# Another order of one period's operations in a convolution and Fourier-mixing kernel on one core

## The chip, the cores and the metric

The kernel runs on one core of one Trainium2 chip. A core has five engines that follow their own instruction streams: TensorE (PE in the profile; its weight loads appear as PEld), VectorE (DVE), ScalarE (ACT), GpSimd (POOL) and SyncE (SP). They meet at semaphores. The metric is the device time of one execution in microseconds (us); lower is better.

## The reference

Two layers on x, 4 x 256 x 256 x 64, all in float32. The change touches layer 0 alone:

```python
h = _pw(_ln(x, g1, b1), w_te, b_te)
F = jnp.fft.fft2(h.astype(jnp.complex64), axes=(1, 2))
fr = jnp.concatenate([jnp.real(F), jnp.imag(F)], axis=-1)
fc = jax.nn.gelu(_pw(fr, w_fc, b_fc), approximate=False)
re, im = (fc[..., :HID], fc[..., HID:])
sp = jnp.real(jnp.fft.ifft2(re + 1j * im, axes=(1, 2)))
x1 = x + _pw(sp, w_tp, b_tp)
h2 = _pw(_ln(x1, g2, b2), w_fe, b_fe)
d = lax.conv_general_dilated(h2, w_dw, window_strides=(1, 1), padding='SAME', dimension_numbers=('NHWC', 'HWIO', 'NHWC'), feature_group_count=HID) + b_dw
d = jax.nn.gelu(d, approximate=False)
return x1 + _pw(d, w_fp, b_fp)
```

`_ln` is a layer normalisation over the 64 channels and `_pw` a matrix product over channels. Layer 1 adds a moving average along time and a truncated Fourier mixing of it; the kernel does that with one 256 x 256 matrix per channel, after layer 0 has ended.

## The kernel before

**Three streams.** Layer 0 is cut into three streams of small operations, each with a short name in the code. A *stream index* says to which piece of the data an instance belongs.

- Forward transform (names in f, and y0, y1, yt0, yt1): loads x, normalises it, folds it by symmetry, and multiplies it on PE with Fourier tables along the first image axis. fx is the scaling by the reciprocal deviation (xt, POOL, line 410), fh0 and fh1 the POOL half sums (xb, line 609, after DVE's lines 582 and 602), y0 and y1 the PE products (line 615), yt0 and yt1 their evictions by ACT (line 633).
- Spectral pairs (x, xs, m, gc, b, g, p, z, zs, w, zt, and u, us, uc, uf for the way back): the second axis of the transform (x, line 725), the mixing of spectra with its GELU (m and p on PE, line 750; b on DVE, line 770; gc on ACT, line 764; g on ACT, line 775), the folding of its result (p0 and p1, POOL, line 781), the products with w_tp (z, PE, line 805), transposes (zt, PE, line 823, with an ACT copy at line 833), and the inverse transform (u, PE, line 856; evictions us, uc and uf at lines 873, 887, 888 and 907).
- Convolution chunks, 128 in number, 32 for an image: load x and u, add the inverse transform (s, PE, line 1041; r0 and r1, DVE, lines 1054 and 1062), normalise (cx: xn, POOL, line 410), transpose (t0 and t1, PE, line 1088; tt0 and tt1, ACT, lines 1098 to 1100), form sums of neighbouring rows (T0: POOL, lines 1124, 1125, 1128; T1: POOL, lines 1131 and 1132; written to td), multiply by the convolution's weights, combine, apply GELU (a0, a1: ACT, line 1276), multiply by w_fp (o0, o1: PE, line 1283), transpose back (ft, line 1308), add and store (st, DVE, line 1322).

**The products of a chunk.** The 3x3 convolution and the product before it are merged into six sums of products. `products` (line 1166) does the 128-row part and `products_beside` (line 1180) the 64-row part. The six are split in two: FIRST (k 1, 2, 3, 4; operations gm and gh) and REST (k 0, 5; operations em and eh). In FIRST, k 1 and 2 go to two single PSUM banks ("FIRST singles", tiles ps_h_c with a 1 in the name) and k 3 and 4 to one double tile, the *pair* (ps_hh_c), of which there is a single buffer. REST goes to two single banks (tiles ps_h_c with a 0). The sums leave PSUM as follows: evict_rest (ec, ACT, line 1200), evict_first (gc_, ACT, lines 1209 and 1212), combine_first (cf0: DVE, lines 1233 and 1234; cf1: DVE, lines 1239 to 1245), add_sums (sp, POOL, lines 1218 and 1223). Line 1245 is the last to read the pair.

**Normalisation.** Forward groups and chunks share one computation of the reciprocal deviation: a seed by integer arithmetic (DVE, line 315), and Newton steps in which ACT squares (lines 354, 364, 375, 395, 396) and POOL multiplies (lines 355, 365, 376, 397). Its result scales xt and xn at line 410.

**What sets the order.** All compute engines run in the order in which the program emits their instructions (a manual schedule, kept in order); DMAs are issued from SP's queue and, for the final output, from ACT's. The program emits in *periods*. `period(n)` goes through a list of names with offsets and calls `do(op, n + offset)`, so that em:-4 in period n is the REST product of chunk n-4 and is the same instance as em:-3 one period before. `do` emits every instance up to the index that hasn't been emitted, and first those that it depends on by two tables, FOLLOWS and EARLY. Before an operation that needs PSUM banks, `make_room` emits what frees one. The place of a name in the list is therefore a wish; what lands on an engine also depends on these tables.

There are four lists. SPECTRUM runs without chunks; FULL (line 1585) runs while all three streams are active, in 60 periods from n = 72 to 131, which emit chunks 0 to 58 (one period, at the border between the first image and the second, has none); MIXED takes over when the forward stream is done, and CONV when only chunks are left. In the trace FULL covers about 824 to 2370 us. `period` selects so:

```python
names = FULL if n < B * FWD + 4 else MIXED if n < CONV_FROM else CONV
```

In FULL the three streams' statistics are done jointly, and some names of the list (fC, fp, fA and others of the forward statistics) emit nothing, as the chunk's operation does their part.

Of the kernel before, what the change touches and what calls it, by code (L numbers as in the profile page):

```python
# [136 lines left out]
def conv_seq_kernel(ctx: ExitStack, tc: tile.TileContext, a: dict, tables: bass.AP, out: bass.AP):  # L137
    nc = tc.nc
    x = a["x"]
# [11 lines left out]
        x="xs", m0="b0", m1="b1", z="zs", w="zt", u="uc", s="r1", t0="tt0", t1="tt1", gm="cf0",  # L151
        em="ec1", o0="fs0", o1="fs1", ft0="st0", ft1="st1", y0="yt0", y1="yt1",
# [1421 lines left out]
    def numbered(text):  # L1574

        return [(w.split(":")[0], int(w.split(":")[1]) if ":" in w else 0) for w in text.split()]

    follows = {}
    for line in FOLLOWS.replace("\n", "|").split("|"):
# [3 lines left out]


    FULL = numbered("""
        g1:-3 em:-4 b0:-2 ec1:-4 cm:-1 gh:-4 m0:-1 ec0:-4 fh1:-3 gc_0:-4 cf0:-4 a0:-5 g0:-2 m1:-1
        p0:-3 fq:-1 p1:-3 z:-3 gc1:-1 fr:-1 gc0:-1 fs0:-5 o0:-5 o1:-5 b1:-1 fa:-3 fs1:-5 fh0:-3
        b0:-1 y0:-3 ft0:-5 g1:-2 fR:-1 sp0:-4 cx:-2 w:-4 ft1:-5 st0:-5 zs:-3 p0:-2 fC:-3 yt0:-3
        cc:-1 xl fm:-1 p1:-2 t1:-2 ul tt1:-2 sp1:-4 fp:-2 fM:-1 s cl fl t0:-2 w:-3 fA:-2 st1:-5
        gc_1:-4 fx:-2 r0 XL tt0:-2 r1 cM:-1 uf:-3 zs:-2 gc1 T0:-2 T1:-2 m1 UL:1 fB:-2 y1:-3 cA:-1 cr  # L1590
        g0:-1 yt1:-3 u:-2 x:2 b1 zt:-4 us:-2 zt:-3 m0 xs:2 cf1:-4 z:-2 x:1 xs:1 gc0 a1:-4 Ta:-2
        cB:-1 fb:-2 cq gm:-3 cC:-1 uc:-2 cR cp:-1 eh:-3
    """)

    MIXED = numbered("""
# [204 lines left out]
```

## Time and profile before

| | us |
|---|---|
| median of 3 runs | 4286.83 |
| lowest and highest | 4285.57, 4288.68 |
| the profiled execution's own time | 4282.18 |
| its span | 4280.0 |
| stage of list FULL, in the trace | about 824 to 2370 |
| one period in its steady part (spacing of DVE's line 1054) | 26.50 |
| one period of MIXED, steady | 23.57 |

The profile is of one execution. Its page gives the busy time of each engine, the chain of work that ended last, and the costliest groups of instructions; the trace can be asked for waits (which instruction of which engine waited for which other, and for how long), for a timeline of one engine and for tables by window. In a timeline the columns are start, duration, engine, line, operation, output and inputs, shapes, the number of merged instructions, and in brackets the idle time ahead with what ended it. The granted TensorE clock of the run was 0.987 of full speed. The costliest groups of the page show how the work is spread:

```profile
L770 DVE TENSOR_TENSOR g<-ps_p,g 128x512 f32<-128x512 f32 x1040 | 703.0, 683 | 127.7 <-ACT g L764 109.4
L781 POOL TENSOR_TENSOR g<-g 128x512 f32<-128x512 f32 (+1 forms) x520 | 674.1, 1312 | 92.8 <-ACT g L775 84.9
L775 ACT ACTIVATE g<-g,b_fc 128x1024 f32<-128x1024 f32 (+1 forms) x520 | 595.2, 1145 | 1.7 <-DVE g L770 1.6
L750 PE MATMUL ps_p<-xs,wp 64*128 64x512 f32 (+1 forms) x2080 | 562.2, 615 | 7.0 <-DVE g L770 3.8
L1166 PE MATMUL ps_h_c<-td,wc_main 128*128 128x256 f32 x2048 | 500.5, 387 | 3.7 <-DVE g L770 1.4
```

After the count come the busy time and the mean duration in ns, and then the idle time of the engine ahead of these instructions with its main releaser.

### The profile page before, as it was taken

To read this page: it belongs to the slowest core of one execution; us is meant where nothing else is said; L and a number is where in the kernel's file an instruction comes from. 1 tells how busy PE (TensorE), PEld (TensorE's weight loads), DVE (VectorE), ACT (ScalarE), POOL (GpSimd) and SP (SyncE) were. 2 spreads that over 40 slices of the span, in tenths; PEclk is the share of its full clock that TensorE was granted. 3 is DMA by queue.
4 is the path that set the end of the run, shared out by engine and by line. 5 is a ranking of instruction groups with operands and counts; after the bars stand their busy time and mean duration, and the time that the engine had idled before them with its cause. 6 is when DMAs were issued, how large, how long until landed. Compare 5 with 4: busy or idle time off the path is not lost.

```text
span 4280.0 us, 67389 instructions
## 1 busy us (share of the span) xinstructions
PE 4123.3 (96%) x22443; PEld 2329.5 (54%) x22443; DVE 3453.5 (81%) x5234; ACT 2962.3 (69%) x5409; POOL 3174.2 (74%) x3156
## 2 busy tenths in 40 slices
PE   8999999889999999899999999999998899999999
PEld 4544444345555555455555556666665566654444
DVE  6968999889999999899999878888886799962222
ACT  3438988778888887788888777888885466641221
POOL 6869999789999988899988877888886688840000
PEclk9999999999999999999999999999999999999999
DMA  6664555535555545445554333444433544439895
GB/s 192 213 192 132 158 159 165 170 99 138 139 138 138 138 138 141 125 132 140 141 141 133 100 106 101 110 108 123 109 99 101 165 114 114 118 109 368 344 342 226
DMA packets 763904, 655.26 MB, mean 153 GB/s; under 512 B 46413, under 2 KB 657695, under 8 KB 755240
## 3 DMA queue, kind: packets, MB, share of 16 engines
q1 hardware_dynamic: 726696, 583.84, 47.0%
q10 hardware_dynamic: 36864, 67.13, 4.1%
q8 instruction: 180, 2.95, 0.3%
q14 instruction: 164, 1.34, 0.1%
HBM read 364.81 MB, written 286.00 MB: 152 GB/s over the span
## 4 chain that ended last, share of the span: by engine, by line
PE 47%; DVE 8%; DMA 2%; POOL 2%; ACT 1%; issue 1%; SPq 0%; DVEq 0%; POOLq 0%; ACTq 0%
PE ps_o L1504 9%; PE ps_h_c L1166 5%; PE ps_p L750 4%; PE ps_h_c L1180 4%; PE ps_f_c L1283 4%; PE ps_s_c L1041 3%; PE ps_hh_c L1166 3%; PE ps_z L805 3%; PE ps_u L856 2%; PE ps_x L725 2%; PE ps_t_c L1088 2%; PE ps_ft_c L1308 2%; PE ps_hh_c L1180 2%; PE ps_zt L823 1%; PE ps_y L615 1%
## 5 line engine op out<-in xcount | busy, mean ns | idle before, releaser
L770 DVE TENSOR_TENSOR g<-ps_p,g 128x512 f32<-128x512 f32 x1040 | 703.0, 683 | 127.7 <-ACT g L764 109.4
L781 POOL TENSOR_TENSOR g<-g 128x512 f32<-128x512 f32 (+1 forms) x520 | 674.1, 1312 | 92.8 <-ACT g L775 84.9
L775 ACT ACTIVATE g<-g,b_fc 128x1024 f32<-128x1024 f32 (+1 forms) x520 | 595.2, 1145 | 1.7 <-DVE g L770 1.6
L750 PE MATMUL ps_p<-xs,wp 64*128 64x512 f32 (+1 forms) x2080 | 562.2, 615 | 7.0 <-DVE g L770 3.8
L1166 PE MATMUL ps_h_c<-td,wc_main 128*128 128x256 f32 x2048 | 500.5, 387 | 3.7 <-DVE g L770 1.4
L1504 PE MATMUL ps_o<-xc,mt 128*128 128x512 f32 x1024 | 441.2, 594 | 2.6 <-DVE oc L1518 2.6
L1166 PEld LDWEIGHTS ps_h_c<-td,wc_main 128*128 128x128 f32 x2048 | 372.6, 192 | 99.3 <-issue 32.1
L764 ACT COPY g<-ps_p 128x512 f32<-128x512 f32 (+1 forms) x520 | 298.5, 589 | 163.3 <-PE ps_p L750 80.7
L1276 ACT ACTIVATE h_c<-h_c,b_conv 128x1024 f32<-128x1024 f32 x256 | 296.5, 1160 | 158.1 <-DVE h_c L1245 53.8
L1518 DVE TENSOR_SCALAR oc<-ps_o,b_fp 128x512 f32<-128x512 f32 x128 | 93.6, 749 | 348.0 <-DMA out_dram<-oc 177.4
L1516 ACT ACTIVATE oc<-ps_o,b_fp 128x512 f32<-128x512 f32 x128 | 86.4, 686 | 359.4 <-PE ps_o L1504 202.8
L1128 POOL TENSOR_TENSOR td<-tt 128x512 f32<-128x512 f32 x256 | 326.9, 1298 | 10.0
L1504 PEld LDWEIGHTS ps_o<-xc,mt 128*128 128x128 f32 x1024 | 194.9, 191 | 248.3 <-issue 236.2
L609 POOL TENSOR_TENSOR xb<-xt 128x512 f32<-128x512 f32 x224 | 284.9, 1279 | 54.9 <-DVE xt L602 36.6
L750 PEld LDWEIGHTS ps_p<-xs,wp 64*128 64x128 f32 x2080 | 191.7, 186 | 235.7 <-issue 84.2
L805 PE MATMUL ps_z<-g,w_tp 128*64 128x512 f32 x1024 | 284.7, 616 | 25.8 <-POOL g L781 13.9
L1322 DVE TENSOR_TENSOR st<-x_c,ps_ft_c 128x256 f32<-128x256 f32 x512 | 260.5, 599 | 36.9 <-PE ps_ft_c L1308 36.8
L725 PEld LDWEIGHTS ps_x<-tab,yb 128*64 128x64 f32 x4064 | 232.7, 137 | 95.7 <-issue 38.3
L1180 PE MATMUL ps_h_c<-td,wc_half 64*128 64x256 f32 (+1 forms) x2048 | 278.9, 396 | 2.3 <-POOL td L1132 1.0
L615 PE MATMUL ps_y<-xb,tab 128*64 128x512 f32 x1024 | 270.6, 614 | 10.8 <-POOL xb L609 9.2
L1283 PE MATMUL ps_f_c<-h_c,w_fp 128*64 128x512 f32 x1024 | 266.1, 614 | 15.2 <-ACT h_c L1276 15.2
L1041 PE MATMUL ps_s_c<-uc_c,tab 64*128 64x512 f32 x1024 | 260.4, 612 | 16.6 <-DVE uc_c L990 11.2
(201 smaller groups left out, 9588.2 us busy)
## 6 DMA issues: line engine op xcount, KB each, us to landing
y_d<-yt SPq DMA_DIRECT2D x256, 256.0 KB, 3.6
yb<-y_d SPq DMA_DIRECT2D x256, 256.0 KB, 4.2
u_d<-ut SPq DMA_DIRECT2D x256, 256.0 KB, 3.6
x_c<-in_x_dram SPq DMA_DIRECT2D x512, 128.0 KB, 3.6
x_d<-st SPq DMA_DIRECT2D x128, 512.0 KB, 5.1
xc<-x_d SPq DMA_DIRECT2D x64, 1024.0 KB, 8.3
out_dram<-oc ACTq DMA_DIRECT2D x256, 256.0 KB, 5.7
xt<-in_x_dram SPq DMA_DIRECT2D x504, 128.0 KB, 2.5
```

What stands on the lines that cost most here:

```text
L725: nc.tensor.matmul(ps[r * C : (r + 1) * C, j * N + t * P : j * N + (t + 1) * P], blk[:, t, k, r * C : (r + 1) * C], tb[:, t, :], start=Tru ...
L750: nc.tensor.matmul(ps[:, :nf], wp[rows, cols], rhs[rows], start=True, stop=r == 1 or not pr["special"],)
L770: nc.vector.tensor_tensor(gt[:, i], re, gt[:, 1], op)
L775: nc.scalar.activation(g, g, AF.Gelu, bias=b_fc[:, half : half + 1])
L781: nc.gpsimd.tensor_tensor(g[:, 0], g[:, 0], g[:, 1], op)
L805: nc.tensor.matmul(ps[r * C : (r + 1) * C, :nf], w_tp, d[:, :nf], start=True, stop=True)
L1041: nc.tensor.matmul(pss[i], tb[i * C : (i + 1) * C], uc[i * C : (i + 1) * C, ::-1, 1 - r, :] if down else uc[i * C : (i + 1) * C, :, r, :], ...
L1128: tt_(new[:, k : k + 3 : 2], a_c, nb_e, op)
L1166: nc.tensor.matmul(product(j, k, par), wc_main[:, par, k, :], td[:, k, slots(j)].rearrange("p j q -> p (j q)"), start=k in (0, 1, 3), stop ...
L1180: nc.tensor.matmul(product(j, k, par)[:, dst.start * Q : dst.stop * Q], wc_half[lo : lo + C, k, :], td[lo : lo + C, k, src].rearrange("p j ...
L1283: nc.tensor.matmul(ps[par * C : (par + 1) * C], w_fp, gs[j][:, :, par, i0 : i0 + 2, :].rearrange("p r j q -> p r (j q)"), start=True, stop ...
L1504: nc.tensor.matmul(ps[:, :nf], mts[i // CM][:, i % CM, t, to * P : (to + 1) * P], xc[:, t, :, :, i, :], start=t == 0, stop=t == 1,)
```

## The change

The list FULL holds the same names with another order; for one of them the offset moves by one with its place (em:-4 near the start of the list becomes em:-3 near its end). No other line differs.

```diff
     FULL = numbered("""
-        g1:-3 em:-4 b0:-2 ec1:-4 cm:-1 gh:-4 m0:-1 ec0:-4 fh1:-3 gc_0:-4 cf0:-4 a0:-5 g0:-2 m1:-1
-        p0:-3 fq:-1 p1:-3 z:-3 gc1:-1 fr:-1 gc0:-1 fs0:-5 o0:-5 o1:-5 b1:-1 fa:-3 fs1:-5 fh0:-3
-        b0:-1 y0:-3 ft0:-5 g1:-2 fR:-1 sp0:-4 cx:-2 w:-4 ft1:-5 st0:-5 zs:-3 p0:-2 fC:-3 yt0:-3
-        cc:-1 xl fm:-1 p1:-2 t1:-2 ul tt1:-2 sp1:-4 fp:-2 fM:-1 s cl fl t0:-2 w:-3 fA:-2 st1:-5
-        gc_1:-4 fx:-2 r0 XL tt0:-2 r1 cM:-1 uf:-3 zs:-2 gc1 T0:-2 T1:-2 m1 UL:1 fB:-2 y1:-3 cA:-1 cr
-        g0:-1 yt1:-3 u:-2 x:2 b1 zt:-4 us:-2 zt:-3 m0 xs:2 cf1:-4 z:-2 x:1 xs:1 gc0 a1:-4 Ta:-2
-        cB:-1 fb:-2 cq gm:-3 cC:-1 uc:-2 cR cp:-1 eh:-3
+        g1:-3 b0:-2 ec1:-4 cm:-1 gh:-4 m0:-1 cf0:-4 a0:-5 g0:-2 fC:-3 p0:-3 m1:-1 fq:-1 p1:-3 z:-3
+        ec0:-4 fh1:-3 fp:-2 gc1:-1 fr:-1 gc0:-1 gc_0:-4 o0:-5 fs0:-5 o1:-5 b1:-1 y0:-3 fa:-3 fs1:-5
+        fh0:-3 b0:-1 ft0:-5 g1:-2 fR:-1 sp0:-4 cx:-2 w:-4 ft1:-5 st0:-5 p0:-2 zs:-3 yt0:-3 cc:-1 xl
+        ul tt1:-2 fM:-1 s XL fm:-1 t0:-2 w:-3 st1:-5 p1:-2 t1:-2 cl fA:-2 fx:-2 fl gc_1:-4 r0 tt0:-2
+        r1 cM:-1 uf:-3 zs:-2 sp1:-4 m1 gc1 T0:-2 g0:-1 yt1:-3 u:-2 T1:-2 cr fB:-2 x:2 b1 cA:-1 zt:-4
+        us:-2 zt:-3 xs:2 z:-2 x:1 xs:1 gc0 em:-3 a1:-4 UL:1 y1:-3 Ta:-2 m0 fb:-2 cB:-1 cq gm:-3
+        cC:-1 cf1:-4 uc:-2 cR cp:-1 eh:-3
     """)
```

## The prediction, made before the changed kernel was run

> **What bounds the kernel now.** I read the page's busy table first, then the waits of the stage that the list governs (about 824 to 2370 us: 60 periods, one convolution chunk each), then its timeline by engine.
>
> ```profile
> PE 4123.3 (96%) x22443; PEld 2329.5 (54%) x22443; DVE 3453.5 (81%) x5234; ACT 2962.3 (69%) x5409; POOL 3174.2 (74%) x3156
> 1000.00:1050.00 50.00, 49.78 (x303) 28.23 (x300) 47.16 (x71) 42.83 (x82) 44.99 (x42) 1.00 0.53 147
> PEld ps_hh_c L1166 <- DVE h_c L1245: 28.2, 48, 2.3
> ```
>
> The second line is a 50 us window of that stage (busy us of PE, PEld, DVE, ACT, POOL; clock; DMA). PE looks full, yet the third line (waits of 900 to 2300 us: total, times, longest) has it wait in 48 periods at the pair product hh, for L1245, the last reader of the pair's only PSUM tile. Anchoring every period at the start of DVE's L1054 gives a steady period of 26.50 us (26.46 to 26.53; chunks 6 to 27 and 38 to 56). So the obvious reading is a PE bound with a wait of 28.2/48 = 0.6 us. A waiting matmul hides in modelled ends, so I compare block lengths instead: FIRST singles and hh take 2.10 and 1.83 us here, 1.83 and 1.73 where the wait is absent (period 29). PE loses 0.27 to 0.37 a period; its own cycle is about 26.13.
>
> One period of the other engines shows a second closed loop:
>
> ```profile
> 1997.42 1.10 POOL L1124 TENSOR_TENSOR tt<-tt 128x512 f32<-128x512 f32 x1
> 1998.60 2.23 POOL L1125 TENSOR_TENSOR tt<-tt 128x512 f32<-128x512 f32 x1
> 2006.13 0.70 POOL L355 TENSOR_TENSOR newton_c<-newton_c,var_c 128x32 f32<-128x32 f32 x1
> 2009.67 0.25 POOL L397 TENSOR_TENSOR rstd_c<-newton_c,rstd_c 128x32 f32<-128x32 f32 x1 [0.85 <-ACT newton_c L396]
> 2023.92 1.10 POOL L1124 TENSOR_TENSOR tt<-tt 128x512 f32<-128x512 f32 x1
> ```
>
> ```profile
> 1997.87 0.69 DVE L315 TENSOR_SCALAR seed_c<-var_c 128x32 int32<-128x32 int32 x1
> 1998.48 1.21 DVE L907 SCALAR_TENSOR_TENSOR ut<-ut,ut 128x1024 f32<-128x1024 f32 x1
> 2005.32 0.68 DVE L1245 SCALAR_TENSOR_TENSOR h_c<-ps_hh_c,s_c 128x512 f32<-128x512 f32 x1
> 2005.91 1.46 DVE L582 TENSOR_TENSOR xb<-xt 128x512 f32<-128x512 f32 x2
> 2016.02 2.74 DVE L770 TENSOR_TENSOR g<-ps_p,g 128x512 f32<-128x512 f32 x4 [0.93 <-ACT g L764]
> ```
>
> DVE's tiny L315 takes 0.69: it ends when POOL's L1124 ends (1998.5). Then POOL's L1125 takes 2.23 instead of about 1.1: it gets going when DVE's L907 ends (1999.7). DVE works without a gap from there to the first L582 (over at about 2006.7), and L355 (0.70 instead of 0.25) ends just after it. After three Newton steps to and fro with ACT, POOL works without a gap to the next L1124. Median lengths of the loop: L1124's end to L907's end 1.15; to L355's end 7.14; Newton to L397's end 3.10; POOL's contiguous work to L1124's end 15.11. The sum is 26.50, the period itself. PE fits into this loop; its wait at hh is a consequence.
>
> ```profile
> L315 DVE TENSOR_SCALAR seed_c<-var_c x51: 176/705/1136, 949.7 to 2342.3; 128x32 int32<-128x32 int32 x50, 128x16 int32<-128x16 int32 x1
> ```
>
> That view of L315 (min/median/max ns) shows that the hold-up is the rule, median 705 against 176 when free. A perturbation tests the loop: in period 22 one Newton gap is 0.30 longer, and period 23 is 26.79 with L1245 and hh late by the same 0.3.
>
> **What the Trainium skill says.** "SBUF — State Buffer", section "Who interferes with whom": DVE and GpSimd share a port pair as an exclusive lock held for the whole instruction, so that the first to issue runs and the other blocks in full. The trace agrees: L315 0.70 against 0.18, L1125 2.23 against 1.1. "Perfetto Trace Analysis", section "Tensor Engine Instruction", warns that TensorE's ends are estimates; here PE is 49.78 of 50 us "busy" while it waits. "TensorE: Matmul & The Clock Gate", Part 1, has the clock halve after idling for about 3.4 us; here half-clock stretches of 6.83 us follow idle gaps of 4.54 and 5.69 in the ramp.
>
> **The change, part by part.** I compared the order of instructions on each engine in the two built programs. Counts are equal everywhere. In 57 periods:
>
> 1. PE: the eight REST main products (1.82 us) move from after FIRST singles and hh to before both. hh starts 1.8 later in PE's order, and its wait of about 0.3 is gone with 1.5 to spare. FIRST singles come 1.8 later too, but their readers (DVE's L1233 at +17 us from the anchor, ACT's L1209/L1212) need the half products beside them, which end at +16.2 and aren't moved; REST's eviction L1200 likewise. REST starts at +8.6 now instead of +12.6; its td was written by POOL's L1132 a whole period before. At that place it takes PSUM tiles that ACT empties, as FIRST does there now (the waits view has L1166 wait 9.9 us for ACT's L740 in 13 cases, and this stays). Cost 0; if REST found its own tiles occupied, it would cost up to what hh's wait costs now, 0.3.
> 2. ACT: L354 (square of the seed) moves three places back, after L775, L633 and L833. Its user L355 starts at +10.8, over 4 us later. 0, and 0.3 us of loss only if ACT were 4 us late.
> 3. POOL: L609, L781, L781, L609 becomes L781, L781, L609, L609, equal work (5.1 us). z gets its g 1.25 us earlier, y its xb's second half at the same time. L1218 and L410 (xt) change places: xt 1.28 earlier, L1218's reader L1244 is at +9.4 against its end at about +2.1. 0 on POOL itself, whose sum stays 15.11.
> 4. DVE and SP: only at the batch boundary (1665 to 1690 us). Two u evictions (L887/888/907 of ut, some 5 us) go behind L770 and L1239 to L1245; SP's spectral output and y loads go ahead of the u stores. The store queue is waited for only by loads five or more us later: 0, at worst 2 us once.
>
> So the steady gain isn't the wait of 0.3; the loop doesn't contain PE. It comes by a side way. With hh free, PE runs ahead by up to 0.7 to 0.8 until t_1 waits for xn (POOL's L410 ends at +23.08, t_1 starts at +23.96). DVE's anchor L1054 follows PE, but no further than its own predecessors let it, about 0.53 (the L315 slack: 0.70 less 0.17). L315 then arrives at +2.0, before L1124 starts (+2.10), so L315 is done before L1124 or slips in at its start; L907 comes up just after L1124 has begun and waits for it. That order is seen in the ramp, in this pair of answers:
>
> ```profile
> 922.10 0.40 DVE L315 TENSOR_SCALAR seed_c<-var_c 128x32 int32<-128x32 int32 x1
> 922.42 2.17 DVE L907 SCALAR_TENSOR_TENSOR ut<-ut,ut 128x1024 f32<-128x1024 f32 x1
> ```
> ```profile
> 922.43 1.08 POOL L1124 TENSOR_TENSOR tt<-tt 128x512 f32<-128x512 f32 x1
> 923.59 2.14 POOL L1125 TENSOR_TENSOR tt<-tt 128x512 f32<-128x512 f32 x1
> ```
>
> There L907 ends 2.16 after L1124's start, against 2.26 in the steady period: 0.10 a period, for about 44 periods 4.4 us. Bounds: nothing (L315 still behind L1124), or 0.37 (PE's own cycle becomes the period).
>
> Transitions, once each:
>
> ```profile
> 859.15 3.19 PE L805 MATMUL ps_z<-g,w_tp 128*64 128x512 f32 x4 [4.54 <-POOL g L781]
> 1681.21 1.99 PE L1166 MATMUL ps_hh_c<-td,wc_main 128*128 128x256 f32 x8 [1.86 <-DVE h_c L1245]
> 1771.80 2.35 PE L805 MATMUL ps_z<-g,w_tp 128*64 128x512 f32 x3 [8.20 <-DVE var_c L294]
> ```
>
> In the ramp z gets g 1.25 earlier, but y then waits for the unmoved second L609; I take 0.9 from the stall of PE at 889.8. At the boundary hh's 1.86 and an h wait of 1.41 go, as combine_first runs before the u evictions, with 0.3 from PE's order: 3.5. Of the 8.20 wait, L609 ahead of the fold accounts for 1.25, a tenth of which I keep back: 1.1. Sum 5.5, bounds 0 and 8.
>
> Total 4.4 + 5.5 = 9.9, so the profiled execution of 4282.18 (span 4280.0) would be 4272. The median shown, 4286.83, is 4.65 above it; I carry that over: **4277 us**.
>
> **Rivals.** *PE was the bound after all:* periods fall to 26.13, 0.37 x 44 = 16.3, and 5.5: 4265. For it: the 48 waits. Against: the loop sums to the period, and period 23. *The wait just moves:* PE waits at t_1 for xn, the loop stays at 26.50, only 5.5 is left: 4281. For it: xn's slack is only 0.88 and xn isn't moved. *Slower:* the same lead brings DVE's L907 to the shared port before POOL's L1124. Then L1124 is held for 1.2, all of POOL moves back, L1132 meets L582, and L355 ends up to 0.75 later: 0.24 to 0.75 a period, x 44, less 5.5: 4292 to 4314. It decides at about 0.1 us of lead more than I assume. For it: L315 and L907 follow each other directly. Against: POOL's L410 holds the port until L1124, with no gap on POOL.
>
> **How the numbers follow.** Forecast 0.38, PE bound 0.22, moved wait 0.20, slower 0.14, something else 0.06. A change under 0.2% (8.6 us) can't be told from none. The forecast lies close to that bound: 0.24 of it faster, 0.14 same. PE bound: faster. Moved wait: 0.03 faster, 0.17 same. Slower: slower. Else: 0.02 and 0.04. Together 0.51, 0.31, 0.18. The range from 4262 (PE bound with transitions at 8) to 4290 leaves out most of the slower case and little below.
>
> **What would show it.** Right: no wait of hh for L1245; waits of t_1 for xn's L410 instead; L315 at 0.2 to 0.4; L1125 still 2.1 to 2.2; L1054 spaced 26.40. PE bound: 26.1 and no wait on PE. Moved wait: 26.50 with L315 still 0.7. Slower: L1124 at 2.2 to 2.3 and 26.7 or more. The 1771.80 and 1681.21 waits should shrink to 7 and under 0.5. I'd be wrong if ACT's Newton squares came late, or if transitions lost time.

## The result and the profile after

| | us |
|---|---|
| kernel before, median of 20 runs | 4287.98 (4283.08 to 4295.75) |
| kernel after, median of 20 runs | 4281.75 (4275.50 to 4289.64) |
| ratio | 0.9985, 95% interval 0.9978 to 0.9992 |
| profiled execution after: time, span | 4280.15, 4278.4 |
| steady period (spacing of DVE's line 1054), before and after | 26.50, 26.50 |

The change saves 6 us (0.15%, 0.08 to 0.22). The forecast was 10 us less, to 4277, with a range from 4262 to 4290. The rival "the wait just moves" had 4281.

Two views of the changed kernel show what PE does now. The first is the window from 1000 to 1050 us, inside the steady part (busy us of PE, PEld, DVE, ACT, POOL; clock; DMA). The second has two rows of the waits from 900 to 2300 us (total, times, longest):

```profile
1000.00:1050.00 50.00, 49.44 (x304) 28.45 (x300) 48.02 (x71) 42.58 (x83) 44.99 (x43) 1.00 0.52 141
```

```profile
PEld ps_f_c L1283 <- ACT g L764: 54.3, 50, 1.7
...
PE ps_f_c L1283 <- ACT g L764: 11.5, 40, 0.8
```

The wait of hh for L1245 is no longer in the list. In its place PE stands at f (L1283), whose second half needs a PSUM bank that ACT empties at L764. The row of PEld alone proves little (before there was such a row of 38.9, without one of PE itself), but that of PE is new: 11.5 us in 40 periods, 0.29 each. PE's block f is 2.21 us long in the period where it was 1.84: 0.37 lost at f, as much as was lost at hh. The period is as long as it was, so one stall has taken the other's place.

L315's view (min/median/max ns) shows a longer hold-up, not the shorter one that was forecast:

```profile
L315 DVE TENSOR_SCALAR seed_c<-var_c x51: 202/1124/1592, 950.9 to 2339.6; 128x32 int32<-128x32 int32 x50, 128x16 int32<-128x16 int32 x1
```

The loop that the prediction reckoned is still there. The timeline of POOL, then of DVE, in a steady period of after:

```profile
1995.43 1.09 POOL L1124 TENSOR_TENSOR tt<-tt 128x512 f32<-128x512 f32 x1
1996.60 2.23 POOL L1125 TENSOR_TENSOR tt<-tt 128x512 f32<-128x512 f32 x1
2004.13 0.70 POOL L355 TENSOR_TENSOR newton_c<-newton_c,var_c 128x32 f32<-128x32 f32 x1
```

```profile
1995.43 1.12 DVE L315 TENSOR_SCALAR seed_c<-var_c 128x32 int32<-128x32 int32 x1
1996.48 1.21 DVE L907 SCALAR_TENSOR_TENSOR ut<-ut,ut 128x1024 f32<-128x1024 f32 x1
...
2003.91 1.46 DVE L582 TENSOR_TENSOR xb<-xt 128x512 f32<-128x512 f32 x2
```

Before, L315 came 0.45 after L1124 had begun and took 0.69. Now both start at 1995.43, and L1124 goes first: L315 takes 1.12, all of L1124 long, and everything after it (L907, L1125 at 2.23, L355 behind L582) stands to L1124 as it did before. PE and DVE lead POOL by 0.42 more (median), and the lead is spent on waiting for the port.

What was saved must then lie at the transitions:

```profile
859.95 2.35 PE L805 MATMUL ps_z<-g,w_tp 128*64 128x512 f32 x3 [3.31 <-POOL g L781]
1679.90 1.89 PE L1166 MATMUL ps_hh_c<-td,wc_main 128*128 128x256 f32 x8
1686.53 1.98 PE L750 MATMUL ps_p<-xs,wp 64*128 64x512 f32 x6 [1.09 <-DVE g L770]
1696.87 1.99 PE L1041 MATMUL ps_s_c<-uc_c,tab 64*128 64x512 f32 x8 [2.81 <-issue]
1769.72 2.34 PE L805 MATMUL ps_z<-g,w_tp 128*64 128x512 f32 x3 [7.36 <-POOL g L781]
```

These are matmuls of PE with the idle time ahead in brackets. The wait of 4.54 in the ramp is 3.31, the next one fell from 5.69 to 4.44, that of 8.20 is 7.36. At the batch boundary 1.86 ahead of hh and 1.41 ahead of h are gone, 1.09 ahead of p is new, and the wait ahead of s grew from 2.34 to 2.81; the long gap between chunks there (starts of L1054) fell from 59.99 to 58.23.

The two profiled executions alone would not show 6 us: they differ by 2.0. Each execution has stretches at half clock of its own (before has two of 6.83 us in the ramp, after four, 27.3 us together), and even the 826 us ahead of the first chunk, where the program is the same, varied from 826.3 to 832.9 over the profiles of this study. In this pair the ramp even got longer: its first six periods take 148.55 us after the change and 147.52 before, in spite of the shorter waits. The stretch around the boundary (chunks 26 to 38) takes 355.40 instead of 358.13, the two steady stretches 0.5 less together.

A straight line through all timed runs whose clock is on record, with one level for each kernel, one for each of the sessions on different chips and one common slope, gives 2.5 us for each 0.001 of mean clock and leaves 2.1 us of scatter. The column "at equal clock" below is a kernel's difference from before in its own session, with its standard error. The runs of before that stand beside after have no clock on record; for the change the column takes three sessions whose levels of before agree within 0.3 us, and gives -7.1 +- 0.6. In the fourth, that of lead24 and lead48, before itself ran 2.8 us faster, so the error of -7.1 is larger than 0.6 if after's chip differed too; the medians have -6.2. The correction also takes out what a kernel itself does to the clock.

### The profile page after: what moved, and what is told of

It reads as the page before. It is cut to its first block, busy times and chain, and to the rows that moved or that the text cites. A ratio compares the mean times of both kernels' runs of the same rounds, so it can differ in the third digit from the quotient of the medians.

```text
span 4278.4 us, 67389 instructions
## 1 busy us (share of the span) xinstructions
PE 4124.8 (96%) x22443; PEld 2339.7 (55%) x22443; DVE 3474.0 (81%) x5234; ACT 2956.7 (69%) x5409; POOL 3177.0 (74%) x3156
## 4 chain that ended last, share of the span: by engine, by line
PE 61%; DVE 13%; ACT 10%; POOL 5%; DMA 5%; issue 3%; SPq 2%; ACTq 0%; DVEq 0%; POOLq 0%
PE ps_o L1504 9%; PE ps_p L750 7%; PE ps_h_c L1166 5%; PE ps_s_c L1041 5%; PE ps_f_c L1283 4%; PE ps_z L805 4%; PE ps_y L615 4%; PE ps_x L725 4%; PE ps_u L856 3%; PE ps_h_c L1180 3%; PE ps_hh_c L1166 3%; PE ps_zt L823 2%; PE ps_t_c L1088 2%; PE ps_ft_c L1308 2%; ACT sq L279 2%
## 5 line engine op out<-in xcount | busy, mean ns | idle before, releaser
L770 DVE TENSOR_TENSOR g<-ps_p,g 128x512 f32<-128x512 f32 x1040 | 702.5, 683 | 103.5 <-ACT g L764 85.4
L781 POOL TENSOR_TENSOR g<-g 128x512 f32<-128x512 f32 (+1 forms) x520 | 675.9, 1315 | 91.9 <-ACT g L775 82.6
L775 ACT ACTIVATE g<-g,b_fc 128x1024 f32<-128x1024 f32 (+1 forms) x520 | 595.7, 1146 | 2.1 <-DVE g L770 2.1
L764 ACT COPY g<-ps_p 128x512 f32<-128x512 f32 (+1 forms) x520 | 297.8, 587 | 157.9 <-PE ps_p L750 100.0
L609 POOL TENSOR_TENSOR xb<-xt 128x512 f32<-128x512 f32 x224 | 282.6, 1280 | 53.4 <-DVE xt L602 33.7
L1283 PE MATMUL ps_f_c<-h_c,w_fp 128*64 128x512 f32 x1024 | 269.9, 615 | 27.2 <-ACT h_c L1276 15.5
```

The source lines that it names most:

```text
L770: nc.vector.tensor_tensor(gt[:, i], re, gt[:, 1], op)
L775: nc.scalar.activation(g, g, AF.Gelu, bias=b_fc[:, half : half + 1])
L781: nc.gpsimd.tensor_tensor(g[:, 0], g[:, 0], g[:, 1], op)
L1283: nc.tensor.matmul(ps[par * C : (par + 1) * C], w_fp, gs[j][:, :, par, i0 : i0 + 2, :].rearrange("p r j q -> p r (j q)"), start=True, stop ...
```

## The experiments

| kernel | median, us | ratio to before, 95% interval | at equal clock, us | steady period |
|---|---|---|---|---|
| after | 4281.75 | 0.9985 (0.9978 to 0.9992) | -7.1 +- 0.6 | 26.50 |
| em_only | 4282.64 | 0.9988 (0.9980 to 0.9996) | -4.3 +- 0.7 | 26.51 |
| no_em | 4287.19 | 0.9993 (0.9985 to 1.0002) | -5.0 +- 0.7 | 26.50 |
| fold_only | 4285.55 | 0.9993 (0.9986 to 0.9999) | -2.0 +- 0.6 | 26.53 |
| after_uf | 4265.20 | 0.9947 (0.9933 to 0.9960) | -22.0 +- 1.0 | 26.12 and 26.3 to 26.6 |
| after_uf2 | 4264.83 | 0.9941 (0.9929 to 0.9954) | -22.0 +- 1.0 | 26.11 to 26.29, two longer |
| before_uf | 4269.48 | 0.9951 (0.9939 to 0.9964) | -18.9 +- 1.0 | 26.12 and 26.3 to 26.5 |
| after_fq | 4286.94 | 0.9992 (0.9984 to 1.0000) | -1.6 +- 0.7 | 26.57 |
| after_w | 4310.55 | 1.0050 (1.0036 to 1.0063) | +23.6 +- 1.0 | 27.10 |
| lead24 | 4278.05 | 0.9986 (0.9977 to 0.9994) | -7.7 +- 0.7 | 26.51 |
| lead48 | 4280.46 | 0.9986 (0.9979 to 0.9993) | -9.1 +- 0.6 | 26.50 |
| half_sq | 4278.88 | 0.9968 (0.9954 to 0.9982) | -9.0 +- 1.2 | 26.44 |

**The change in two parts.** Each part was built alone; no other engine's compute order moves in em_only, and no_em is all the rest.

```diff
 em_only, from before
-        g1:-3 em:-4 b0:-2 ...
+        g1:-3 b0:-2 ...
-        ... xs:1 gc0 a1:-4 Ta:-2
+        ... xs:1 gc0 em:-3 a1:-4 Ta:-2
 no_em, from after
-        g1:-3 b0:-2 ...
+        g1:-3 em:-4 b0:-2 ...
-        us:-2 zt:-3 xs:2 z:-2 x:1 xs:1 gc0 em:-3 a1:-4 ...
+        us:-2 zt:-3 xs:2 z:-2 x:1 xs:1 gc0 a1:-4 ...
```

> The kernel before with one part of the change: REST main products ahead of FIRST and hh on PE; nothing moves on any other engine. Loop theory (POOL, DVE and ACT close a loop of 26.50 us without PE): the steady period stays 26.50, the wait of hh for L1245 is gone, PE waits 0.3 to 0.4 a period at another place instead, the anchor L1054 leads POOL by 0.3 to 0.45 more; the time is within 2 us of before. PE theory: period 26.1 and 16 us less. If the measured 6 us of the change come from this part, the time is 5 to 7 us less.

> The kernel after with REST main products put back behind FIRST and hh: all of the change but its part on PE. If the gain of 6 us is made at the transitions by the moved folds and the u evictions behind combine_first at the batch boundary: 4 to 6 us less than before, steady period 26.50 with hh's wait of 0.3 back. If PE's part made the gain: within 2 us of before.

At equal clock em_only took 4 us and the rest 5; together they give 9, the change has 7 (the difference of 2 is within twice its error). The medians split it otherwise, 6.3 and 1.8, and the interval of no_em's ratio includes 1; so em_only saves either way, but what the rest saves shows at equal clock only. In em_only the period stays 26.51 though hh's wait is gone; the PE theory's 26.1 is out. The 4 us of this part were more than the "within 2" that the loop theory expected. Its profile shows 2 of them at transitions: 0.3 less over the first ramp, all of it in the last period (26.53 for 26.93), 0.3 over the ramp behind the boundary, whose last period has the same 0.4 less (PE may take up its lead there, once each), and 1.1 at the boundary (58.86 for 59.99), where hh no longer waits.

**The folds alone.** POOL's two L781 go ahead of the first L609:

```diff
 fold_only, from before
-        ... ec0:-4 fh1:-3 gc_0:-4 ... p1:-3 z:-3 gc1:-1
+        ... ec0:-4 gc_0:-4 ... p1:-3 z:-3 fh1:-3 gc1:-1
```

> The kernel before with one part of the change: POOL's two folds L781 ahead of the first L609; nothing else moves. PE's waits of 4.54 and 5.69 at z in the ramp fall by 1.25 each, the 8.20 by 0.8, and the stretches at half clock behind the first two are 3.4 us shorter, so 2 to 3 us less than before; steady period 26.50 with hh's wait kept. If the folds bring nothing, as y waits for the second L609 in any case: within 1 us of before, and the 4 to 5 us of the kernel with all but PE's part come from the batch boundary.

2.0 +- 0.6 us less (2.9 in the medians). In its profile the first three periods of the ramp take 63.5 us instead of 65.8, and the two half-clock stretches there are 3.41 us each instead of 6.83. The fourth gives 0.5 back, with a new half-clock stretch of 3.41 in it and the fifth. What no_em saves beyond this, 3.0 +- 0.9, is left for its other edits: ACT's L354, POOL's exchange of L1218 and L410, and the u evictions at the batch boundary. They were not built alone, so that share is a difference and not a measurement, and where it lies isn't shown: in no_em's profile the gap at the boundary is 61.67, longer than before, with 8.3 us of it at half clock.

**Is it the loop?** The sharpest test takes L907/L920 (u's last combination on DVE) away from L1125, whose port it holds, and leaves the change otherwise as it is:

```diff
 after_uf, from after
-        r1 cM:-1 uf:-3 zs:-2 ...
+        r1 cM:-1 zs:-2 ...
-        cC:-1 cf1:-4 uc:-2 cR cp:-1 eh:-3
+        cC:-1 cf1:-4 uf:-3 uc:-2 cR cp:-1 eh:-3
```

> The kernel after with DVE's L907/L920 moved from behind L315 to behind L602, so that it no longer holds up POOL's L1125. Loop theory: L1125 falls from 2.23 to about 1.1, the loop would be 25.4 to 25.6, and PE's own cycle is the next bound: period 26.0 to 26.2, 14 to 22 us less than the kernel after. If the loop isn't what bounds (PE by some other wait, or ACT): period stays 26.50 and the time that of after.

16.6 us less than after in the medians (15 at equal clock), though no instruction was removed and PE's order is the same. L1125 of after_uf, in a view of that line (min/median/max ns), and the DVE instruction that now follows L315:

```profile
L1125 POOL TENSOR_TENSOR tt<-tt x52: 1272/1279/1289, 950.5 to 2330.8; 128x512 f32<-128x512 f32 x52
```

```profile
2014.59 0.44 DVE L315 TENSOR_SCALAR seed_c<-var_c 128x32 int32<-128x32 int32 x1
2014.94 1.21 DVE L283 TENSOR_REDUCE total_c<-x_c 128x16 f32<-128x1024 f32 x1
```

L1125 takes 1.28 in every period; in the profiles of before and after its median is 2.23. About every second period is 26.12, which agrees with PE's own cycle as the prediction had it from block lengths (26.13). The others are 0.2 to 0.5 longer. In those L315 comes just behind L1124's start and is held again, but that this lengthens them is not shown: in after_uf2, below, L315 is held in nearly every period (median 1.02) and no second period is long.

The same edit in the kernel before, and another place for L907 (just ahead of L582) in the kernel after:

```diff
 before_uf, from before
-        gc_1:-4 fx:-2 r0 XL tt0:-2 r1 cM:-1 uf:-3 zs:-2 ...
+        gc_1:-4 fx:-2 r0 XL tt0:-2 r1 cM:-1 zs:-2 ...
-        cB:-1 fb:-2 cq gm:-3 cC:-1 uc:-2 cR cp:-1 eh:-3
+        cB:-1 fb:-2 cq gm:-3 cC:-1 uf:-3 uc:-2 cR cp:-1 eh:-3
 after_uf2, from after
-        r1 cM:-1 uf:-3 zs:-2 ... Ta:-2 m0 fb:-2 cB:-1 ...
+        r1 cM:-1 zs:-2 ... Ta:-2 m0 uf:-3 fb:-2 cB:-1 ...
```

> The kernel before with DVE's L907/L920 moved from behind L315 to behind L602, as in after_uf, and nothing of the change. Loop theory: period 26.1 to 26.3 as there, the wait of hh for L1245 gone or below 0.1 by itself since L1245 comes 1.1 us earlier, 14 to 18 us less than before; the distance to after_uf is that of the transitions, 3 to 7 us. If hh's wait were what bounds the kernel before: no change of the period, or less than 0.1.

> The kernel after with DVE's L907/L920 moved from behind L315 to just before the two L582 (behind L1245), instead of behind L602. Loop theory: L1125 short as in the other place, but L907 now lies in the loop's path on DVE ahead of L582 and may hold POOL's L1132 or L355: DVE's path from L1124's end to L582's end is as long as in the kernel after (about 7.1), so the period falls only by the part of 1.15 that POOL gets back; 26.12 to 26.5, and the time between that of after and 18 us less. A PE bound of 26.12 in every period would mean that the other place lost its 0.2 to 0.5 in every second period to L907 before L376.

before_uf keeps hh ahead of REST, and its period falls to 26.12 and 26.3 to 26.5 all the same. The wait of PEld's hh for L1245 falls from 28.2 us in 48 periods to 4.2 in 3, though nothing was moved on PE: hh's wait was a consequence of the loop. The distance to after_uf, 3.1 +- 1.4 at equal clock, is at the low end of what was expected. after_uf2 has no slow second periods; the two places can't be told apart in time (0.0 +- 1.4). Both after_uf and after_uf2 are faster than before and after.

**The step that failed: who reaches the port first.** The forecast had L315 done before L1124, or slipping in at its start. Four kernels try to give it a longer lead, and none does it in the way intended. In the first two other waits came up:

```diff
 after_fq, from after
-        ... p0:-3 m1:-1 fq:-1 p1:-3 z:-3
+        ... p0:-3 m1:-1 p1:-3 z:-3
-        ec0:-4 fh1:-3 fp:-2 gc1:-1 fr:-1 gc0:-1 gc_0:-4 ...
+        ec0:-4 fh1:-3 fp:-2 gc1:-1 gc0:-1 fq:-1 fr:-1 gc_0:-4 ...
 after_w, from after
-        ... cx:-2 w:-4 ft1:-5 st0:-5 p0:-2 zs:-3 yt0:-3 ...
+        ... cx:-2 ft1:-5 st0:-5 p0:-2 yt0:-3 ...
-        ul tt1:-2 fM:-1 s XL fm:-1 t0:-2 w:-3 st1:-5 ...
+        ul tt1:-2 fM:-1 s w:-4 zs:-3 XL fm:-1 t0:-2 st1:-5 ...
-        ... g0:-1 yt1:-3 u:-2 T1:-2 ...
+        ... g0:-1 yt1:-3 w:-3 u:-2 T1:-2 ...
```

> The kernel after with ACT's square L279 (of xt) moved behind the two evictions L764, which free a PSUM bank of f 0.95 us sooner; only ACT's order changes. It tests the step of the forecast that failed: PE's lead of 0.42 was too small. With 0.1 to 0.5 more lead L315 comes before L1124 starts. Forecast's mechanism: L315 0.2 to 0.4, L907 ends 2.16 after L1124's start, period 26.40, 4 to 5 us less than after. Rival: L907 takes the port before L1124, L1124 takes 2.2, period 26.7 to 27.2, 10 to 30 us more. Neither: period 26.50.

> The kernel after with both transposes zt (L823) moved on PE behind t_1 and s, and ACT's zs (L813) moved along; it takes 0.44 us out of the path from PE's f to DVE's L1054, so that L315 comes 0.4 us earlier against POOL's L1124 than in the kernel after. It tests the step of the forecast that failed, by a lead of 0.8 in place of 0.42. Forecast's mechanism (L315 slips in ahead of L1124, L907 ends 2.16 after L1124's start): L315 0.2 to 0.6, period 26.40, 3 to 5 us less than after. Rival: L907 gets the port ahead of L1124 and POOL is held up: 26.7 to 27.2, 10 to 30 us more. Or L315 stays behind L1124 all the same: 26.50 and the time of after.

In after_fq L764 did not come earlier, as it now waits for PE's z (40.9 us in 51 waits), and everything behind L279 on ACT came later, the copies tt (L1099) included; L1124 begins just 0.08 after L1099's end there, so probably waits for it. L315 came 0.30 behind L1124's start: the lead shrank. after_w met the price of the slower rival, with a cause of its own, seen in POOL's and DVE's timelines:

```profile
2047.77 0.18 DVE L315 TENSOR_SCALAR seed_c<-var_c 128x32 int32<-128x32 int32 x1
2047.85 1.22 DVE L920 TENSOR_TENSOR ut<-ut,ut 128x1024 f32<-128x1024 f32 x1
```

```profile
2048.26 1.77 POOL L1124 TENSOR_TENSOR tt<-tt 128x512 f32<-128x512 f32 x1 [0.77 <-ACT tt L1099]
2050.10 1.29 POOL L1125 TENSOR_TENSOR tt<-tt 128x512 f32<-128x512 f32 x1
```

The moved zs (L813) put ACT's copies of tt back, so L1124 was 0.77 late, and DVE took the port for L920 meanwhile. L1124 then stood behind it and took 1.77. Period 27.10, 29 us more than after in the medians. That shows what it costs POOL to lose the port, but L315 was ahead because L1124 was late, and not by a lead of its own.

The other two take work out of PE, between f and L1054, in the product s; what they leave out is missing in the sum for the odd residual:

```diff
 lead48, from after
-            down = quarters[j[1] // (NCH // 4)][2]
+            down, cut = quarters[j[1] // (NCH // 4)][2], j[0] * NCH + j[1] < 59
 ...
-                for i in range(2):
+                for i in range(2 - (cut and r == 0)):
 ...
-                        start=r == 0,
+                        start=r == 0 or (cut and i == 1),
 lead24: as this, but 256 of the 512 columns instead of none
```

> The kernel after with less work on PE in the product s (L1041) of chunks 0 to 58: of the first term for the second bank only 256 of 512 columns are computed, so the sum for the odd residual lacks the others. PE gets 0.24 us shorter between f and L1054, no engine's order moves. PE's lead over POOL grows from 0.42 to 0.66, so L315 comes 0.24 before L1124's start, while POOL is in L1218. Forecast's mechanism: L315 (0.2 to 0.6) goes ahead of L1124 or in between, L907 ends 2.16 after L1124's start, period 26.40. If POOL's instructions that follow each other without a gap keep the port: L315 about 1.36, L1125 2.23, period 26.50 as after, though PE has 0.24 less to do. Slower rival: L907 before L1124, L1124 2.2, period 26.7 or more.

> As lead24, with the first term for the second bank left out altogether in chunks 0 to 58: 0.48 us less on PE between f and L1054, L315 0.48 before L1124's start. Forecast's mechanism: period 26.40. POOL keeps the port: L315 about 1.6, 26.50. Slower rival: 26.7 to 27.2. If PE's time counted in the steady period, it would fall below 26.1 in one of the two.

The period stayed at 26.51 and 26.50, and L315 still began with L1124, within 0.02 us in the median, in both. So PE's time doesn't count in the steady part, up to 0.48 us, and it isn't PE that limits the lead. Measured against before on the same chip they gain about as much as after does (the ratios are 0.9986, 0.9986 and 0.9985). In the trace of after ACT has no gap from L396 to L764, and then DVE none above 0.10 from L770 to L315:

```profile
2007.20 0.32 ACT L396 ACTIVATE newton_c<-newton_c,affine 128x32 f32<-128x32 f32 x1
2007.42 1.14 ACT L775 ACTIVATE g<-g,b_fc 128x1024 f32<-128x1024 f32 x1
2008.46 1.05 ACT L1200 COPY h_c<-ps_h_c 128x512 f32<-128x512 f32 x2
...
2012.02 1.07 ACT L279 ACTIVATE sq<-xt 128x1024 f32<-128x1024 f32 x1
2012.98 1.07 ACT L764 COPY g<-ps_p 128x512 f32<-128x512 f32 x2
```

Before, L1200 waited 0.30 there for PE's half products (16.7 us in 47 waits; 4.2 in 6 after). From L396's start to L1054's start it is 12.62 us before, and 12.20 or 12.21 in after, em_only, lead24 and lead48 (medians). The last experiment shortens this chain instead; it squares only 8 of 16 rows, so the forward group's variance lacks the other squares:

```diff
 half_sq, from after
-            nc.scalar.activation(sq[:, :, 0:C], src(j), AF.Square)
+            n = ROWS // 2 if joint["on"] and side == 0 else ROWS
+            nc.scalar.activation(sq[:, :n, 0:C], src(j)[:, :n], AF.Square)
```

> The kernel after with less work on ACT: while list FULL runs, the squares L279 of the forward group cover 8 of 16 rows, so its variances are made of half the new squares. With PE shortened by 0.24 and 0.48 the lead stayed at 0.42, so it isn't PE that limits it; the trace of after shows ACT without a gap from L396 to L764 and DVE without a gap from L770 to L315. Half of L279 takes 0.4 to 0.5 out of that chain. Theory: the lead grows by 0.3 to 0.45 and L315 comes while POOL is in L1218, ahead of L1124's start. Forecast's mechanism then: L315 ahead of L1124, L907 ends 2.16 after L1124's start, period 26.40. POOL keeps the port between instructions without a gap: L315 1.4 to 1.6, period 26.50. Slower: L907 takes the port, L1124 2.2, 26.7 or more. If the chain of ACT and DVE isn't what limits the lead: L315 still starts together with L1124.

DVE and POOL of half_sq in a steady period:

```profile
2025.97 0.41 DVE L315 TENSOR_SCALAR seed_c<-var_c 128x32 int32<-128x32 int32 x1
2026.30 2.18 DVE L920 TENSOR_TENSOR ut<-ut,ut 128x1024 f32<-128x1024 f32 x1
```

```profile
2025.08 1.27 POOL L1218 TENSOR_TENSOR h_c<-h_c,s_c 128x512 f32<-128x512 f32 x1
2026.31 1.09 POOL L1124 TENSOR_TENSOR tt<-tt 128x512 f32<-128x512 f32 x1
2027.48 2.14 POOL L1125 TENSOR_TENSOR tt<-tt 128x512 f32<-128x512 f32 x1
```

With L315 0.34 ahead of L1124's start it waits for the end of L1218 only and goes in between; L920 finds the port taken and ends 2.17 after L1124's start. The period is 26.44. This is the picture that the forecast drew for the change, with 2.16 and 26.40.

The changed kernel itself has this picture in three of 39 steady periods. There L1124 happens to come late by about 0.1, and L315, 0.11 to 0.13 ahead of it, takes 0.20 to 0.23. One of them, on DVE and on POOL:

```profile
1295.46 0.20 DVE L315 TENSOR_SCALAR seed_c<-var_c 128x32 int32<-128x32 int32 x1
```

```profile
1295.56 1.10 POOL L1124 TENSOR_TENSOR tt<-tt 128x512 f32<-128x512 f32 x1
```

L907 ends 2.19 after L1124's start there, instead of 2.26. So a tenth of a microsecond of lead was missing.

## Why the prediction was partly right

**What bounds the steady part: right.** The loop of POOL, DVE and ACT at 26.50 carries it in before and after. Moving one two-input DVE operation out of it gave 16.6 us; taking hh's wait out or shortening PE by 0.24 and 0.48 gave nothing there.

**Step 1 (PE): right in its cost, and the wait went elsewhere.** REST ahead of FIRST costs nothing, hh's wait is gone. The lead of PE was to end at t_1 waiting for xn; it ended earlier, at f waiting for L764.

**Steps 2 and 3 (ACT's L354, POOL's swaps): right.** L355 is still released by L582, not by L354, and POOL's contiguous work from L397's end to L1124's end is 15.11 as before.

**The side way: the failed step.** "DVE's anchor L1054 follows PE, but no further than its own predecessors let it, about 0.53": the lead was 0.42. The 0.53 was read off L315's hold-up on DVE. The true limit was the chain ahead of it: ACT's gap of 0.30 at L1200, and some 0.1 by which L1200 now starts before L775's end. With 0.42 L315 arrives when L1124 starts, and loses to it; so of 0.10 a period, 4.4 us in all, nothing came. half_sq and the three periods of after show that the mechanism itself works once the lead is there. Its size was taken too large as well: half_sq's period is 0.06 shorter, and the steady stretches that the prediction names hold about 40 periods, not 44.

**Transitions: 5.5 predicted, 7.1 +- 0.6 measured at equal clock, 6.2 in the medians.** The ramp's waits shrank by 1.23 and 1.25, as forecast. For the folds the prediction had 2.0, 0.9 in the ramp and 1.1 at the wait of 8.20, and fold_only measured 2.0 +- 0.6 in all; the split is not shown. The boundary was over-estimated: 1.8 in the pair of traces instead of 3.5, because p and s waited for 1.6 us of what hh and h gave up. The wait of 8.20 fell by 0.84 instead of 1.1. The 0.4 by which the last period of each ramp is shorter in after, as in em_only, was not in the sum. Folds, boundary and the two ramps make about 4.6 us; where the other 2.5 lie stays open.

**The number: partly luck.** Of the 9.9 us, the steady 4.4 did not come at all. That the change still saves 6 us is owed to transitions that gave a little more than their 5.5.

**The rivals.** The moved wait came true in its number (4281) and its main sign, a period of 26.50 with only the transitions' gain, so it describes the steady part better than the forecast does. It had the place of the wait wrong (t_1 instead of f), and L315 at 0.7 instead of 1.12. The PE bound is excluded by em_only, lead24 and lead48. The slower one did not come in the change; after_w shows a price of its size where L1124 is late for another reason.

## What to carry to other kernels

A wait that PE shows in every period may only be where PE falls into step with a loop of other engines: sum the loop, and compare block lengths, before a wait's total is booked as gain. When a step turns on which of two engines comes first, follow both back to a common ancestor and compare the two contiguous chains; slack that is read at the end of one of them isn't yet lead. And an operation that blocks a neighbour in such a loop is worth moving even if nothing waits for it: here that was 16.6 us, where the reordering of PE gave nothing in the steady part.

## What the runs showed of the hardware that was not expected

In the steady part of after, em_only, lead24 and lead48, L315 and L1124 start within 0.04 us of each other in 146 of 156 periods, and POOL goes first each time: L315 takes 1.10 to 1.16. In seven periods L315 is 0.11 to 0.27 ahead, and DVE goes first: it takes 0.20 to 0.36. With 0.34 us of lead DVE gets in between two POOL instructions that follow each other without a gap (half_sq, L315 0.41). So a queue of POOL instructions did not keep the port here: DVE got it at the end of one, when it was already waiting.

Shorter PE gaps went with shorter stretches at half clock, but not always. At PE's first wait for L781 in the ramp, the three profiles with a gap of about 4.54 us (before, em_only, before_uf) have 6.83 us at half clock; in before the stretch begins 2.6 us into the gap. Of the ten with a gap of about 3.31, eight have 3.41 and two have 10.24; one of these two is the changed kernel's own. What decides it is not shown.
